# Projecting self-attention's values in PE tiles of 64 rows by 32 columns

## The chip, the cores and the metric

The kernel runs on one NeuronCore of a Trainium2 chip. Five engines work side by side, each with its own list of instructions: TensorE (PE in the profile, its weight loads PEld), VectorE (DVE), ScalarE (ACT), GpSimd (POOL) and SyncE (SP), which issues most DMAs. They wait for each other through semaphores only. The metric is the device time of one execution in microseconds (us). Before the change it is 1100.89 us, the median of three runs (1097.67, 1102.98 and 1100.89).

## The reference

A transformer block in float32 with batch 2, 1024 tokens of 256 features, and a context of 154 tokens of 192 features per batch. Self-attention, cross-attention and a gated feed-forward part follow each other, each behind a layer norm and with a residual sum:

```
h = layernorm(x, ln1);  x = attention(h, h, sa_wq, sa_wk, sa_wv, sa_wo, sa_bo) + x
h = layernorm(x, ln2);  x = attention(h, cond, ca_wq, ca_wk, ca_wv, ca_wo, ca_bo) + x
h = layernorm(x, ln3);  p = h @ ff_w1 + ff_b1
x = (p[:, :1024] * gelu(p[:, 1024:])) @ ff_w2 + ff_b2 + x
```

`attention` has 16 heads of 64: `q`, `k` and `v` are products with 256 x 1024 weights, the scores are scaled by 1/8 and go through a softmax, and the weighted values are multiplied by `wo`. The change is about one product alone, `v = h @ sa_wv` of self-attention.

## The kernel before

**Units and periods.** Self-attention goes by 16 units: 2 batches by 8 pairs of heads (128 columns of `q`, `k` and `v` each). A unit has eight periods (`for p in range(SA)` in the main loop, SA = 128 periods). In a period PE computes the scores of two groups of queries (`scores`, L482, matmuls at L489, tile `s`), then one block of other work: the weighted values of the half unit before (`weigh`, L528, matmuls at L535, tile `po`), or a projection for the next unit (`project_both`, L351, matmuls at L358: `pq_sa`, `pk_sa`; `project_self_values`, L383, matmuls at L389: `pv_sa`), and where there is room a piece of the output projection (L463, `py_sa`) or four transposes of a layer norm (L276, `ph_ln`). The order is written out by hand: `run_work` (L559) takes the next projection from a list, and the program's order on each engine is the order in which the Python code emits.

**Behind the scores.** DVE takes the maximum over each score tile (L650, tile `st`), ACT exponentiates (L500, tile `p`), SP exchanges the halves' maxima and sums by four small DMAs (L510), POOL joins and scales (L518 to L525, L600), and DVE transposes the weights (L614, tile `pT`) for `po`. There are two score tiles in PSUM, and a period uses both: the scores of the next period wait until ACT has read these.

**PE's tiles.** A matmul here names a tile of the array by rows (what is summed over) and columns (what comes out in PSUM's partitions); matmuls in different tiles can run side by side. Scores, `po`, `pq_sa` and `pk_sa` use tiles of 64 rows by 32 columns, eight in the array. `pv_sa` uses 64 rows by 128 columns, two in the array. Each has the two halves of the tokens in the two halves of the partitions: row tile `r` takes its 64 partitions of the normalised activations `h` and writes into its own PSUM bank `pv[r]`.

**The value projection.** For each of the four tiles of 128 tokens in a half (`i`) it sums over four chunks of 64 features (`c`, NH = 4), with the tokens as the stationary operand (128 columns) and 128 columns of `sa_wv` streamed past. That is 4 x 4 x 2 = 32 matmuls a unit. A float32 matmul shows as two records in the trace, one for each of two passes, each with its weight load: 64 records a unit, 1,024 in all. The first unit's block is done in two halves of two token tiles each. Then ACT copies both banks into `v_sa` (L398), and two DMAs (L405, L406) put the other half of the partitions beside. `po` of the next unit reads `v_sa`.

Of the kernel before, what the change touches and what calls it, by code (L numbers as in the profile page):

```python
# [13 lines left out]
P = 128  # L14
# [4 lines left out]
def tile_transformer_block(ctx: ExitStack, tc: tile.TileContext, a: dict, out: bass.AP):  # L19
    nc = tc.nc  # L20
# [15 lines left out]
    HR = P // 2  # L36
    NH = D // HR
    CC = DC // 2
    KP = T // 2
    KB = 32  # L40
# [56 lines left out]
    row_of, r = {}, 0  # L97
# [69 lines left out]
    for n in names[2:]:  # L167
        own = rows[row_of[n] - n_cols:row_of[n] - n_cols + n_of[n], :]
# [214 lines left out]
    def project_self_values(v, pv, wt, h, i0, n, soon):  # L383

        for i in range(i0, i0 + n):
            for c in range(NH):
                for r in range(2):
                    own = slice(r * HR, (r + 1) * HR)
                    nc.tensor.matmul(  # L389
                        pv[r][:, i * P:(i + 1) * P], lhsT=h[own, c, i * P:(i + 1) * P],  # L390
                        rhs=wt[own, c, :], start=(c == 0), stop=(c == NH - 1),
                        tile_position=(r * HR, 0),
                    )

        def store():
            tiles = [slice(r * GT + i0, r * GT + i0 + n) for r in range(2)]
            for r in range(2):
                nc.scalar.copy(  # L398
                    v[:, tiles[r], 0, :],
                    pv[r][:, i0 * P:(i0 + n) * P].rearrange("p (t d) -> p t d", d=P))  # L400
            if i0 + n == GT:
                move()

        def other_half():
            nc.sync.dma_start(out=v[:QG, :, 1, :], in_=v[QG:, :, 0, :])  # L405
            nc.sync.dma_start(out=v[QG:, :, 1, :], in_=v[:QG, :, 0, :])  # L406

        def move():
            if soon:
                other_half()  # L410
            else:
                later.append(other_half)

        return store
# [33 lines left out]
    def value_pieces(b, pr, parts, soon=True):  # L448
        n = GT // parts
        return [  # L450
            costing(2, lambda i=i: project_self_values(
                qk["sa", b, pr][2], two_banks(f"pv_sa{b}_{pr}_{i}"), wsl["sa", pr, "v"],
                hT["sa", b], i * n, n, soon))
            for i in range(parts)
        ]
# [626 lines left out]
    with tc.manual_schedule():  # L1082
# [11 lines left out]
        own = [ps_s.tile([P, 2, HB], F32, tag="s", name=f"first_{r}") for r in range(2)]  # L1094
# [45 lines left out]
        for p in range(SA):  # L1140
# [20 lines left out]
            h, hg = divmod(p, SH)  # L1161
            if h == 0 or hg < LAG:
# [5 lines left out]
                f = (ui - NPAIR // 2 - 1) * EC  # L1168
# [107 lines left out]
        for k in range(2 * FU):  # L1276
            c = CA + k
# [59 lines left out]
```

## Time and profile before

The profiled execution took 1098.87 us, and its span, from the first instruction of the program to the last, is 1097.1 us.

| what | busy us (share) | instructions |
|---|---|---|
| PE | 1076.0 (98%) | 18388 |
| PEld | 711.9 (65%) | 18388 |
| DVE | 893.2 (81%) | 1301 |
| ACT | 638.1 (58%) | 2057 |
| POOL | 730.1 (67%) | 1552 |
| `pv_sa` on PE (L389) | 62.0 | 1024 |
| scores on PE (L489) | 260.2 | 4096 |
| `po` on PE (L535) | 239.1 | 8192 |

Self-attention fills the span up to about 700 us, cross-attention overlaps its end, and the feed-forward part is last. A line of a group of instructions reads: source line, engine, operation, tile written and tiles read, for PE the tile of the array (`64*32` is 64 rows by 32 columns) and the streamed operand, the count; then busy time in us and the mean duration of one in ns; then the idle time before them and what ended it. Busy times are those of overlapping records taken together. A record's duration includes the time that a matmul needs to pass through the array, so that records of different tiles overlap, and costs are better read from the start of one block of matmuls to the start of the next.

### The profile page before, as it was taken

What the parts mean: (1) busy time and instruction counts of PE and PEld (TensorE: products, weight loads), DVE (VectorE), ACT (ScalarE), POOL (GpSimd) and SP (SyncE); (2) the same over time, 40 slices, a digit from 0 to 9 for tenths busy, and PEclk for the clock granted to TensorE, in tenths of its full rate; (3) what the DMA queues carried; (4) which work ended last, traced back from release to release, by engine and by line L of the source; (5) the groups of instructions that cost most, each with busy time, mean ns of one, the idle gap of its engine ahead of it and who ended that gap; (6) DMA issues with size and microseconds to landing.
All of it is one profiled execution on the core that took longest, in us unless ns stands there. A gap on an engine that the chain in (4) does not pass through costs nothing.

```text
span 1097.1 us, 44912 instructions
## 1 busy us (share of the span) xinstructions
PE 1076.0 (98%) x18388; PEld 711.9 (65%) x18388; DVE 893.2 (81%) x1301; ACT 638.1 (58%) x2057; POOL 730.1 (67%) x1552
## 2 busy tenths in 40 slices
PE   8999999999999999999999999899999999899998
PEld 6555656556766565566575666566766677688887
DVE  5888999898989998999999989978877877644442
ACT  5666766667666666666776775666555554232221
POOL 2676777777777777777776777776756785565331
PEclk9999999999999999999999999999999999999999
DMA  3222112122111011111110210136665545000000
GB/s 82 67 57 57 46 43 52 42 49 46 35 41 45 20 42 33 38 42 24 42 42 19 47 33 18 28 99 157 170 154 124 116 106 116 1 10 14 12 15 29
DMA packets 104094, 60.71 MB, mean 55 GB/s; under 512 B 32330, under 2 KB 94674, under 8 KB 103890
## 3 DMA queue, kind: packets, MB, share of 16 engines
q1 hardware_dynamic: 102514, 57.07, 21.9%
q8 instruction: 145, 2.38, 0.9%
q10 hardware_dynamic: 1376, 0.79, 0.2%
q14 instruction: 59, 0.48, 0.2%
HBM read 27.91 MB, written 2.10 MB: 27 GB/s over the span
## 4 chain that ended last, share of the span: by engine, by line
PE 72%; ACT 7%; DMA 5%; DVE 5%; POOL 5%; SPq 3%; issue 3%; DVEq 0%; POOLq 0%; ACTq 0%
PE po L535 14%; PE s L489 14%; ACT p L500 6%; PE pf L1065 5%; PE py_ca L463 5%; DMA st<-st 5%; PE py_sa L463 4%; PE pq_ca L358 4%; PE poc L877 4%; PE pb L999 4%; PE pv_sa L389 3%; PE pk_sa L358 3%; DVE st L650 3%; PE sc L798 3%; SPq L510 3%
## 5 line engine op out<-in xcount | busy, mean ns | idle before, releaser
L500 ACT ACTIVATE p<-s,st 128x512 f32<-128x512 f32 x512 | 344.8, 686 | 195.8 <-DVE st L650 183.2
L600 POOL TENSOR_SCALAR p<-p,rd,ee 128x512 f32<-128x512 f32 x512 | 385.7, 767 | 47.7 <-DVE rd L596 46.7
L650 DVE TENSOR_REDUCE st<-s 128x2 f32<-128x1024 f32 x256 | 300.7, 1215 | 23.6 <-PE s L489 11.1
L614 DVE STREAM_TRANSPOSE pT<-p 128x1024 f32<-128x1024 f32 x256 | 302.2, 1217 | 0.2 <-POOL p L600 0.2
L489 PE MATMUL s<-k_sa,q_sa 64*32 64x512 f32 x4096 | 260.2, 592 | 8.8 <-ACT p L500 7.8
L535 PE MATMUL po<-pT,v_sa 64*32 64x256 f32 x8192 | 239.1, 376 | 0.7 <-DVE pT L614 0.7
L535 PEld LDWEIGHTS po<-pT,v_sa 64*32 64x32 f32 x8192 | 173.5, 106 | 75.1 <-issue 20.3
L489 PEld LDWEIGHTS s<-k_sa,q_sa 64*32 64x32 f32 x4096 | 80.8, 106 | 114.3 <-ACT p L500 58.7
L814 ACT ACTIVATE p<-sc,neg 128x154 f32<-128x154 f32 x256 | 96.2, 405 | 84.2 <-DVE rden L822 81.0
L825 POOL TENSOR_SCALAR p<-p,rden 128x154 f32<-128x154 f32 x256 | 96.8, 398 | 59.4 <-DVE rden L822 58.9
L500 ACT ACTIVATION_READ_ACCUMULATOR p<-s,st 128x1 f32 x512 | 103.8, 203 | 0.0
L523 POOL TENSOR_TENSOR zz<-ee,st 128x8 f32<-128x8 f32 x128 | 25.9, 202 | 73.1 <-ACT ee L521 73.1
L389 PEld LDWEIGHTS pv_sa<-sa_wv,hT_ln 64*128 64x128 f32 x1024 | 58.8, 188 | 14.6 <-DMA sa_wq<-in_L_xattn_sa_wq_dram 5.0
L389 PE MATMUL pv_sa<-sa_wv,hT_ln 64*128 64x128 f32 x1024 | 62.0, 275 | 0.3 <-ACT v_sa L398 0.3
L463 PE MATMUL py_ca<-ca_wo,o_ca 128*128 128x256 f32 x256 | 60.0, 382 | 0.5 <-DVE o_ca L890 0.5
L518 POOL TENSOR_TENSOR dd<-st 128x8 f32<-128x8 f32 x128 | 25.5, 199 | 52.0 <-DMA st<-st 47.6
L463 PE MATMUL py_sa<-sa_wo,o_sa 128*128 128x256 f32 x256 | 59.7, 385 | 0.0
L463 PEld LDWEIGHTS py_sa<-sa_wo,o_sa 128*128 128x128 f32 x256 | 47.3, 190 | 17.8 <-issue 6.2
L358 PE MATMUL pq_sa<-hT_ln,sa_wq 64*32 64x512 f32 (+1 forms) x976 | 57.9, 586 | 0.0
L358 PE MATMUL pq_ca<-hT_ln,ca_wq 64*128 64x512 f32 (+1 forms) x304 | 57.8, 590 | 0.0
L803 DVE TENSOR_REDUCE neg<-sc 128x6 f32<-128x924 f32 (+1 forms) x48 | 47.8, 998 | 11.9 <-PE sc L798 11.8
L358 PE MATMUL pk_sa<-hT_ln,sa_wk 64*32 64x512 f32 x960 | 57.3, 591 | 0.0
(117 smaller groups left out, 1454.5 us busy)
## 6 DMA issues: line engine op xcount, KB each, us to landing
wf<-pT_ca SPq DMA_DIRECT2D x128, 128.0 KB, 2.4
st<-st SPq DMA_DIRECT2D x512, 1.0 KB, 1.8
v_sa<-v_sa SPq DMA_DIRECT2D x32, 256.0 KB, 3.8
sa_wq<-in_L_xattn_sa_wq_dram SPq DMA_DIRECT2D x32, 128.0 KB, 3.5
sa_wk<-in_L_xattn_sa_wk_dram SPq DMA_DIRECT2D x32, 128.0 KB, 2.9
sa_wv<-in_L_xattn_sa_wv_dram SPq DMA_DIRECT2D x32, 128.0 KB, 3.2
ca_wq<-in_L_xattn_ca_wq_dram SPq DMA_DIRECT2D x32, 128.0 KB, 3.9
wf<-in_L_xattn_ff_w_dram SPq DMA_DIRECT2D x12, 256.0 KB
```

What stands on the lines that cost most here:

```text
L358: nc.tensor.matmul(pq[r][f:f + m, at:at + n], lhsT=wt[own, c, f:f + m], rhs=h[own, c, t0:t0 + n], start=(c == 0), stop=(c == NH - 1), tile ...
L389: nc.tensor.matmul(pv[r][:, i * P:(i + 1) * P], lhsT=h[own, c, i * P:(i + 1) * P], rhs=wt[own, c, :], start=(c == 0), stop=(c == NH - 1), ...
L463: nc.tensor.matmul(py[:, e * D:(e + 1) * D], lhsT=o[:, i, (t + e) * P:(t + e + 1) * P], rhs=wo[kind][:, g * HP + i, :], start=(i == 0), st ...
L489: nc.tensor.matmul(sc[a4 * KB:(a4 + 1) * KB, j, :], lhsT=q[r, c:c + KB], rhs=k[r, h * HB:(h + 1) * HB], start=True, stop=True, tile_positi ...
L500: nc.scalar.activation(pr[:, j, :], sc[:, j, :], AF.Exp, bias=st[:, 0, 0, i, j:j + 1], accum_out=st[:, 0, 1, i, j:j + 1],)
L535: nc.tensor.matmul(po[a2][d:d + KB, :QH // 2], lhsT=v[r, t, e, d:d + KB], rhs=pT[r, d // DH * NK + n, :], start=(t == 0 and e == 0), stop= ...
L600: nc.gpsimd.tensor_scalar(pr[:, j, :], pr[:, j, :], rd[:, c:c + 1], ee[:, 0, c:c + 1], op0=ALU.mult, op1=ALU.mult,)
L614: nc.vector.transpose(halves[h][:, :, c:c + KB], groups.pop(0).rearrange("p j (n k) -> p (j n) k", k=KB))
L650: nc.vector.tensor_reduce(st[:, 0, 0, i, :], sc[i], AX.X, ALU.max, negate=True)
L814: nc.scalar.activation(pr_[:, j, i, :T], sc[:, j, i * T:(i + 1) * T], AF.Exp, bias=neg[:, j, i:i + 1], accum_out=den[:, j, i:i + 1],)
L825: nc.gpsimd.tensor_scalar(pr_[:, j, i, :T], pr_[:, j, i, :T], rden[:, j, i:i + 1], 1.0, op0=ALU.mult, op1=ALU.mult,)
L1065: nc.tensor.matmul(own[:, :D], lhsT=ub[pair][j][:, f, e * P:(e + 1) * P], rhs=w2[:, f, :], start=(f == 0), stop=(f == NF - 1),)
```

## The change

The matmuls of the value projection are cut into tiles of 64 rows by 32 columns: the 128 tokens of the stationary operand are loaded as four times 32 columns, and each quarter writes its 32 partitions of the same PSUM bank. The streamed operand, its 128 columns and the sum over `c` stay. There are four times as many matmuls, 128 a unit; the two row tiles and the four column tiles follow each other in the order that `project_both` has. Nothing else is changed: what the copies and DMAs behind it do is the same.

```
         for i in range(i0, i0 + n):
             for c in range(NH):
-                for r in range(2):
-                    own = slice(r * HR, (r + 1) * HR)
-                    nc.tensor.matmul(
-                        pv[r][:, i * P:(i + 1) * P], lhsT=h[own, c, i * P:(i + 1) * P],
-                        rhs=wt[own, c, :], start=(c == 0), stop=(c == NH - 1),
-                        tile_position=(r * HR, 0),
-                    )
+                for f in range(0, P, KB):
+                    for r in range(2):
+                        own = slice(r * HR, (r + 1) * HR)
+                        nc.tensor.matmul(
+                            pv[r][f:f + KB, i * P:(i + 1) * P],
+                            lhsT=h[own, c, i * P + f:i * P + f + KB],
+                            rhs=wt[own, c, :], start=(c == 0), stop=(c == NH - 1),
+                            tile_position=(r * HR, f),
+                        )
```

`P` is 128, `HR` 64 and `KB` 32.

## The prediction

> **What bounds the kernel now.** I read the page first, then the groups of instructions with shapes kept apart, the chain of waits through one stretch of the self-attention stage, the timeline around two value projections, the list of who waited for whom, and last a table of stretches between value projections.
>
> The page's busy times and the groups by shape:
>
> ```profile
> PE 1076.0 (98%) x18388; PEld 711.9 (65%) x18388; DVE 893.2 (81%) x1301; ACT 638.1 (58%) x2057; POOL 730.1 (67%) x1552
> ...
> L535 PE MATMUL po<-pT,v_sa 64*32 64x256 f32 x8192 | 239.1, 376 | 0.7 <-DVE pT L614 0.7
> L389 PE MATMUL pv_sa<-sa_wv,hT_ln 64*128 64x128 f32 x1024 | 62.0, 275 | 0.3 <-ACT v_sa L398 0.3
> ```
>
> PE is busy 98% of the span and waits almost nowhere, so its time is the first suspect. The changed line takes 62.0 us. Each float32 matmul of the code shows as two records: 512 calls stand behind the x1024.
>
> The chain of waits from 300 to 330 us (start, length, what), a stretch in which nothing but PE is on the chain:
>
> ```profile
> 302.62 3.77 PE pv_sa L389 x64
> ...
> 315.17 3.45 PE po L535 x128
> 318.63 1.72 PE s L489 x32
> ```
>
> These lengths are true costs, start to next start. A block in tiles of 64 rows by 32 columns (`64*32`) works through eight tiles side by side: scores, 32 records of 512 columns, are 4 groups of eight at 1.72 / 4 = 0.430 us; `po`, 128 records of 256 columns, is 16 groups at 3.45 / 16 = 0.2156 us. The value projection, 64 records of 128 columns in tiles of 64 rows by 128 columns (`64*128`), is 32 pairs at 3.77 / 32 = 0.118 us.
>
> The timeline of PE alone, at a value projection with scores on both sides:
>
> ```profile
> 43.93 1.93 PE L489 MATMUL s<-k_sa,q_sa 64*32 64x512 f32 x32
> 45.79 3.84 PE L389 MATMUL pv_sa<-sa_wv,hT_ln 64*128 64x128 f32 x64
> 49.56 1.95 PE L489 MATMUL s<-k_sa,q_sa 64*32 64x512 f32 x32
> 51.30 3.01 PE L535 MATMUL po<-pT,v_sa 64*32 64x256 f32 x104
> ```
>
> Scores ahead of the other shape last 45.79 - 43.93 = 1.86 us, those behind it 1.74, against 1.72 between blocks of one shape. So leaving `64*32` costs 0.14 us and entering it 0.02, beside what lies in the 3.77.
>
> Who waited for whom, 40 to 650 us (us in total, times, longest):
>
> ```profile
> ACT p L500 <- DVE st L650: 159.9, 103, 2.8
> ...
> PEld s L489 <- ACT p L500: 46.3, 88, 1.6
> ```
>
> PE's weight loads for the scores wait for the exponentials that still read the old scores, and these for the vector engine's maxima. Most of that is hidden behind the block that PE is running. Where it is not, the table of stretches shows it (PE, PEld, DVE, ACT, POOL busy us with counts, clock, DMA):
>
> ```profile
> 50.00:84.00 34.00, 33.20 (x864) 17.61 (x848) 29.60 (x31) 21.86 (x67) 23.84 (x52) 1.00 0.23 58
> 88.00:128.00 40.00, 38.99 (x912) 21.00 (x908) 36.32 (x42) 26.09 (x79) 28.29 (x61) 1.00 0.21 50
> 132.00:168.00 36.00, 36.00 (x866) 19.96 (x872) 34.63 (x42) 24.36 (x71) 27.27 (x56) 1.00 0.18 41
> ...
> 262.00:302.00 40.00, 40.00 (x936) 27.71 (x936) 35.54 (x40) 27.83 (x83) 30.71 (x65) 1.00 0.19 43
> ...
> 435.00:475.00 40.00, 39.87 (x924) 22.87 (x920) 38.27 (x45) 25.96 (x80) 28.79 (x62) 1.00 0.17 40
> ```
>
> Between the fifteen full blocks PE stands, in order of time, for 0.80, 1.01, 0, 0, 0.49, 0, 0, 0, 0.23, 0.13, 0.24, 0.02, 0.02 and 0 us; DVE is busy up to 38.27 of 40 us. There PE and DVE are nearly equal bounds. The granted clock is 1.00 throughout.
>
> **The change, part by part.**
>
> *Matmuls.* 512 calls become 2,048, so 1,024 records become 4,096; per block 64 become 256, which is 32 groups of eight tiles. The work streamed is the same: a tile's 128 columns pass 32 times either way. The trace has no `64*32` group of 128 columns, so I bound it. From below: the two rows above give (0.430 - 0.2156) / 256 = 0.84 ns a column and almost no fixed part, so 128 columns need 0.2156 - 128 x 0.00084 = 0.108 us. From above: the densest stream of `64*32` matmuls in the trace is `po`, 3.45 / 128 = 27 ns apiece; if the queue cannot issue faster, a group takes 8 x 27 = 0.216 us. Between them decides the one place where PE starts from rest behind a wait. The timelines of weight loads and matmuls from 17.6 us:
>
> ```profile
> 17.69 0.21 PEld L489 LDWEIGHTS s<-k_sa,q_sa 64*32 64x32 f32 x16 [0.81 <-ACT k_sa L381]
> 17.72 0.66 PE L489 MATMUL s<-k_sa,q_sa 64*32 64x512 f32 x8 [0.64 <-DVE k_sa L379]
> ```
>
> Each load lasts 0.106 us by the groups, so sixteen start within 0.21 - 0.106 = 0.10 us, and eight matmuls (0.61 us each here) within 0.05 us. A group of 128 columns needs eight of each in 0.108 us. That is nearer to the lower end; I take 0.1085 us, a block of 32 x 0.1085 = 3.47 us.
>
> Against this speaks the Trainium skill, "TensorE: Matmul & The Clock Gate", Part 1: matmul starts never come closer than about 25 ns, however few the columns. The eight starts within 0.05 us show that this doesn't hold between tiles of one group; whether it holds as a mean over 256 no row shows. By the skill's figure a group would be 8 x 25 = 200 ns and the whole 512 x (0.200 - 0.118) = 42 us slower on PE (an estimate from that page); by the rows above it is not.
>
> *Shape changes.* The 15 full blocks and two half blocks (the first unit's) all follow scores. Seven full ones are followed by scores: each had 0.14 + 3.77 + 0.02 = 3.93 us, and has 3.47: 0.46 us less, of which 0.02 us is rounding that I drop (0.44). Eight are followed by the transposes of the next layer norm (`128*128`), so leaving `64*32` is paid after the block instead of before it: 0.14 + 3.77 against 3.47 + 0.14, 0.30, taken as 0.28. A half block is 0.24 shorter. Sum on PE: 7 x 0.44 + 8 x 0.28 + 2 x 0.24 = 5.8 us.
>
> *What of it reaches the end.* Where PE already stands in the stretch behind a block, the exponentials and behind them DVE set the pace; what PE saves it then waits. I count a block's saving in full where the stretch up to the next block shows no idle PE (the blocks at 128, 170, 259, 303, 346 and 605 us: 0.44 + 0.28 + 0.28 + 0.28 + 0.44 + 0.28 = 2.0), half where it idles 0.02 us, or only at the end of the stage (518, 562 and 648 us: 0.42), and not where it idles 0.13 us or more (46, 84, 214, 389, 432, 475 us) nor in the first unit, whose half blocks are followed by waits for start-up work. Sum 2.4 us. The ends: nothing given back, 5.8; all given back, 0.
>
> *Moved work and queues.* The lists of DVE, ACT, POOL and SP instructions, with their waits, are the same; no DMA is added but instruction loading. The two copies out of PSUM (L398) wait for a block that ends 0.3 to 0.4 us earlier, and behind them is ACT work that PE does not wait for yet.
>
> *Instruction loading.* The page's instruction queue q8 brings 145 packets and 2.38 MB, 16 KB each; over PE's 36,776 records (two times 18,388) that is 254 records a packet, so I take it to be PE's. 6,144 more records are 24 packets more. A packet of `po` lasts 254 records, 3.4 us; in the new block it lasts 1.73 us. Should loading not keep up, PE starves inside the block. Lower end: nothing, as the trace shows no wait for it. Upper end: the difference of 1.7 us lost twice a block, 16 x 3.4 = 54 us. I take nothing, as the nearest row, `po`, runs without a gap, and scores of 1.72 us and 64 + 64 records lie between the dense blocks.
>
> **Sum.** The profiled execution took 1098.87 us (span 1097.1 and 1.8 around it): 1098.87 - 2.4 = 1096.5. The median of the runs, 1100.89, is 2.0 above it, so 1098.5.
>
> **The rivals.**
>
> 1. *Issue binds (slower).* If eight loads and eight matmuls take longer than the columns to stream, the group is as long as their issue. The 5.8 us saved are gone at 0.1085 + 5.8 / 512 = 0.120 us a group. At 0.15 us PE has 512 x 0.0415 - 5.8 = 15 us more work; what waits for exponentials now (PE's idle 3.0 us between the blocks, and the slack that comes with it) would hide up to 5: 1111 to 1116. At `po`'s 0.216 us it is 512 x 0.1075 - 5.8 = 49 us, less up to 15: 1135 to 1150. For it: no stretch of the trace issues this densely for over 0.1 us. Against it: the burst at 17.7 us.
> 2. *Nothing is given back (faster by half a per cent).* 5.8 us, 1095.1. For it: in the stretches without idle PE the whole machine moves with it. Against: six of fourteen stretches show PE standing already.
> 3. *All is given back, or instruction loading eats it.* 1100.9, up to 1106. For it: DVE at 38.27 of 40 us. Against: DVE was below PE in every stretch.
>
> **How the numbers follow.** What a measurement can tell from no change is about 0.5%, 5.5 us. My forecast (a part is kept) 0.48; rival 3, 0.14; rival 2, 0.12; rival 1, 0.26, spread from 0.12 to 0.216 us a group, so that 0.03 of it stays within half a per cent and some 0.12 lies below 1112. So faster 0.12, within 0.5% 0.65, slower 0.23. The range reaches from rival 2 with 1 us of spread, 1094, to 1112, which leaves out the farther half of rival 1. The forecast alone: 1096 to 1101.
>
> **What would show it.** `pv_sa` at 4,096 records with `64*32` 64x128; blocks of 3.47 us from start to next start; scores ahead of them at 1.72 instead of 1.86; PE's wait for exponentials up by some 3 us in the same stretches that have it now. Wrong if blocks last over 3.95 us, or if weight loads of `pv_sa` show idle time put down to issue.

## The result, and the profile after

The changed kernel takes 1125.39 us, the median of four runs (1123.58 to 1129.5), against 1100.58 us for the kernel before in the same comparison: 24.8 us more, a ratio of 1.0239 with a 95% interval of 1.0219 to 1.0258. The forecast was 1098.5 us and the range ended at 1112.

The page's busy times of the kernel after:

```profile
PE 1078.1 (96%) x21460; PEld 709.3 (63%) x21460; DVE 893.3 (80%) x1301; ACT 639.6 (57%) x2057; POOL 730.3 (65%) x1552
```

PE works 2 us longer in a span that is 25 us longer (1121.8 us), at a granted clock of 0.998. So the time has gone into standing still, and the groups of instructions with shapes kept apart, after, say where:

```profile
L390 PE MATMUL pv_sa<-sa_wv,hT_ln 64*32 64x128 f32 x4096 | 68.2, 271 | 23.9 <-issue 23.9
L390 PEld LDWEIGHTS pv_sa<-sa_wv,hT_ln 64*32 64x32 f32 x4096 | 61.0, 105 | 37.7 <-issue 34.7 <-DMA sa_wq<-in_L_xattn_sa_wq_dram 1.6 <-ACT v_sa L400 0.4
L400 ACT COPY v_sa<-pv_sa 128x512 f32<-128x512 f32 x30 | 16.2, 589 | 14.8 <-PE pv_sa L390 14.5
```

Before, PE stood 0.3 us ahead of `pv_sa`. Now it stands 23.9 us there, and no other engine and no DMA ends that idle time: it is put down to issue. ACT's copies, which used to find the block ready (the line of before follows), wait 14.5 us for it.

```profile
L398 ACT COPY v_sa<-pv_sa 128x512 f32<-128x512 f32 x30 | 16.1, 593 | 0.7 <-PE pv_sa L389 0.6
```

The timeline of PE, after, around one value projection (the count is that of the records in the row):

```profile
172.62 0.64 PE L491 MATMUL s<-k_sa,q_sa 64*32 64x512 f32 x8
173.05 3.32 PE L390 MATMUL pv_sa<-sa_wv,hT_ln 64*32 64x128 f32 x215
178.08 0.88 PE L390 MATMUL pv_sa<-sa_wv,hT_ln 64*32 64x128 f32 x41 [1.71 <-issue]
178.88 0.66 PE L276 MATMUL ph_ln<-ident,xn_ln 128*128 128x128 f32 x4
```

The first 215 matmuls stream as the forecast had it: (3.32 - 0.27) / 215 = 14.2 ns apiece, and start to start a group of eight takes 0.109 to 0.110 us wherever PE isn't stopped. Then PE stops for 1.71 us, and the rest comes. The block lasts 178.88 - 173.05 = 5.83 us in place of 3.77. Over the fifteen full blocks it is 4.5 to 6.4 us.

The chain of waits, after, from 128 to 140 us, shows two such stops in one block, and what lies between them:

```profile
127.64 1.43 PE s L491 x24
129.07 1.59 PE pv_sa L390 x113
130.66 0.47 issue
131.13 2.02 PE pv_sa L390 x128
133.14 1.44 issue
134.58 0.44 PE pv_sa L390 x13
```

Between the stops there are 128 matmuls, with their 128 weight loads 256 records: one packet of 16 KB of the instruction queue if a record stands for 64 bytes of it (16,384 / 256). This is not an accident of one block. Where PE's records are numbered from the start of the kernel (matmuls, weight loads and PE's own semaphore instructions), 21 of the 22 stops inside `pv_sa` fall on number 193 or 194 of a run of 256; the 22nd is the 2.3 us between the two halves of the first unit's block, in which PE does other work. At each of the 21 PE goes on 1.3 to 1.5 us after a packet of the queue has arrived, and the next packet starts 1.0 to 2.8 us after that. The page's row of this queue, after:

```profile
q8 instruction: 169, 2.77, 1.0%
```

There are 24 packets more than the 145 before, as forecast. The shortest time from the start of one packet to that of the next is 3.33 us, before it was 3.37. The value block now needs a packet every 1.73 us.

The waits of the same stretch, 40 to 650 us, after (us in total, times, longest):

```profile
PEld s L491 <- issue: 45.3, 157, 1.9
PEld pv_sa L390 <- issue: 29.1, 34, 2.0
...
PEld s L491 <- ACT p L502: 25.9, 55, 1.2
```

PE's wait for the exponentials, 46.3 us before, has gone down, not up by 3: PE now comes late, and finds the scores' tiles free. The loads of the scores, which stand behind seven of the fifteen blocks, wait for issue too: 45.3 us with one wait of 1.9, where before it was 27.6 us and none over 0.3. The stretches show the same turn (columns as before the change):

```profile
88.00:128.00 40.00, 39.09 (x970) 20.66 (x952) 35.70 (x41) 26.21 (x80) 27.40 (x58) 1.00 0.20 47
...
262.00:302.00 40.00, 38.72 (x1027) 22.12 (x1019) 34.24 (x38) 26.68 (x77) 28.60 (x57) 1.00 0.17 38
435.00:475.00 40.00, 37.53 (x1049) 21.89 (x1040) 36.69 (x43) 24.25 (x73) 28.70 (x60) 1.00 0.17 41
```

DVE falls from 38.27 to 36.69 of 40 us in the last of them: nothing behind PE has become the bound.

Two theories stood at this point, named F and I in what follows. F: PE gets no more than one packet of 256 records each 3.3 us or so, and starves in a block that uses them faster. I: loads and matmuls can't be issued this densely, whatever their loading. A second question was open beside it: would the smaller tiles have gained the 2.4 us that the forecast kept, if PE had not starved?

### The profile page after: what moved, and what is told of

Its sections match the earlier page's. It is cut to its first block, busy times and chain, and to the rows that moved or that the text cites. A ratio compares the mean times of both kernels' runs of the same rounds, so it can differ in the third digit from the quotient of the medians.

```text
span 1121.8 us, 51056 instructions
## 1 busy us (share of the span) xinstructions
PE 1078.1 (96%) x21460; PEld 709.3 (63%) x21460; DVE 893.3 (80%) x1301; ACT 639.6 (57%) x2057; POOL 730.3 (65%) x1552
## 4 chain that ended last, share of the span: by engine, by line
PE 75%; ACT 6%; DMA 5%; DVE 4%; issue 4%; POOL 4%; SPq 2%; DVEq 0%; ACTq 0%; POOLq 0%
PE s L491 15%; PE po L537 14%; PE pv_sa L390 5%; ACT p L502 5%; PE pf L1067 5%; PE py_ca L465 5%; DMA st<-st 4%; PE py_sa L465 4%; PE poc L879 4%; PE pq_ca L358 4%; PE pb L1001 3%; PE pk_sa L358 3%; PE pq_sa L358 3%; PE sc L800 3%; DVE st L652 2%
## 5 line engine op out<-in xcount | busy, mean ns | idle before, releaser
L537 PE MATMUL po<-pT,v_sa 64*32 64x256 f32 x8192 | 236.2, 376 | 0.7 <-DVE pT L616 0.7
L537 PEld LDWEIGHTS po<-pT,v_sa 64*32 64x32 f32 x8192 | 170.3, 106 | 77.6 <-issue 26.8
L390 PE MATMUL pv_sa<-sa_wv,hT_ln 64*32 64x128 f32 x4096 | 68.2, 271 | 23.9 <-issue 23.9
L390 PEld LDWEIGHTS pv_sa<-sa_wv,hT_ln 64*32 64x32 f32 x4096 | 61.0, 105 | 37.7 <-issue 34.7
L816 ACT ACTIVATION_READ_ACCUMULATOR p<-sc,neg 128x1 f32 x256 | 56.4, 220 | 0.0
```

Source lines behind the costliest of these rows:

```text
L390: nc.tensor.matmul(pv[r][f:f + KB, i * P:(i + 1) * P], lhsT=h[own, c, i * P + f:i * P + f + KB], rhs=wt[own, c, :], start=(c == 0), stop=( ...
L537: nc.tensor.matmul(po[a2][d:d + KB, :QH // 2], lhsT=v[r, t, e, d:d + KB], rhs=pT[r, d // DH * NK + n, :], start=(t == 0 and e == 0), stop= ...
L816: nc.scalar.activation(pr_[:, j, i, :T], sc[:, j, i * T:(i + 1) * T], AF.Exp, bias=neg[:, j, i:i + 1], accum_out=den[:, j, i:i + 1],)
```

## Experiments on the stops

**The same tiles with half the records.** The value projection in tiles of 64 rows by 32 columns, but 256 columns streamed by each matmul:

```
-        for i in range(i0, i0 + n):
+        for i in range(i0, i0 + n, 2):
             for c in range(NH):
+                c2 = min(c, NH - 2)
...
-                            pv[r][f:f + KB, i * P:(i + 1) * P],
+                            pv[r][f:f + KB, i * P:(i + 2) * P],
...
-                            rhs=wt[own, c, :], start=(c == 0), stop=(c == NH - 1),
+                            rhs=wt[own, c2:c2 + 2, :], start=(c == 0), stop=(c == NH - 1),
```

> The value projection keeps tiles of 64 rows by 32 columns, but streams 256 columns at a time: 1,024 calls instead of 2,048, the same time on the array (16 groups of 0.216 us a block), half the records (256 a block). Left out: the right sum; chunk c is multiplied with weight chunks c and c+1, so the values are not the reference's. Theory F (instruction loading: PE gets 256 records in no less than about 3.4 us): no gap inside the blocks, blocks of about 3.45 us, and the time is what I had forecast for the change, 1096 to 1100, some 2 to 3 us under the kernel before. Theory S (the 64 by 32 shape itself costs here, by weight loads, PSUM or lost clock): blocks stay at 4 us or more and the time over 1110. Theory D (what PE saves is lost at DVE and the exponentials, and more): 1100 or above with blocks of 3.45 us.

It took 1104.4 us, 1.0015 of the kernel before (0.9998 to 1.0032). The group of this kernel:

```profile
L391 PE MATMUL pv_sa<-sa_wv,hT_ln 64*32 64x256 f32 x2048 | 60.4, 376 | 0.5 <-ACT v_sa L401 0.5
```

No stop is left, and blocks last 3.45 us where scores follow at once. So the tiles, the order and the work streamed are innocent, and the number of records is what stops PE. But the saving of about 0.3 us a block does not show in the time: all of it is given back, where 2.4 us was forecast to stay.

**Tiles between the two.** 64 rows by 64 columns, twice the matmuls of before instead of four times (`for f in range(0, P, HR)`, with 64 columns in each load):

> The value projection in tiles of 64 rows by 64 columns: twice the calls of the kernel before (1,024), 256 records a block, 32 groups of four tiles. Theory F: 256 records in some 3.5 us just pass, no gap inside the blocks or one of a few tenths of a us; the change of tile shape is paid as before, so 1098 to 1103. Theory I (each matmul beyond those of before costs its issue, in proportion to their number): a third of the loss of the change for a third of its extra matmuls, 1106 to 1110.

1104.84 us, 1.0016 (0.9999 to 1.0034). Blocks last 3.655 us without a stop, with 256 records each. This is F's number, and also a correct kernel that is no better than before.

**The other way round: more records in `po`.** The kernel before, with the weighted values in two runs of 128 columns instead of one of 256:

```
-        for e in range(2):
+        for e, x in ((e, x) for e in range(2) for x in range(0, QH // 2, P)):
...
-                        po[a2][d:d + KB, :QH // 2],
-                        lhsT=v[r, t, e, d:d + KB], rhs=pT[r, d // DH * NK + n, :],
+                        po[a2][d:d + KB, x:x + P],
+                        lhsT=v[r, t, e, d:d + KB], rhs=pT[r, d // DH * NK + n, x:x + P],
...
```

Among the lines left out is the flag that starts a sum: it is set on the first of the two runs alone.

> The kernel before, with the value projection untouched, but the weighted values streamed in two runs of 128 columns instead of one of 256: 4,096 more calls, 8,192 more matmul records and as many loads, the same columns through the array. Theory F: a block of 512 records takes two loadings, about 6.9 to 7 us instead of 3.45; with the scores' 64 records a period has 576, which need 7.7 us instead of 5.17. Over 64 blocks 2.5 to 3.5 us each: 1260 to 1320. If only the value projection's place or data were slow: at most 1110.

1271.17 us, 1.1521 (1.1457 to 1.1585). Its group, and its instruction queue:

```profile
L535 PE MATMUL po<-pT,v_sa 64*32 64x128 f32 x16384 | 282.8, 272 | 120.3 <-issue 120.1
```

```profile
q8 instruction: 209, 3.42, 1.1%
```

64 packets more cost 1271.2 - 1103.3 (the kernel before in that comparison) = 168 us, 2.6 us each, with 120 us of stops put down to issue. The 64 `po` blocks of 512 records take 3.8 to 8.3 us, 6.0 in the median; with 1.72 us and 64 records of scores that is 2.25 packets in 7.7 us, 3.4 us each. The stops thus follow the records, not the value projection.

**Half of the sum.** The kernel after, with chunks 0 and 2 of the four alone, so that a block has 256 records in tiles of 64 rows by 32 columns with 128 columns:

```
-            for c in range(NH):
+            for c in range(0, NH, 2):
...
-                            rhs=wt[own, c, :], start=(c == 0), stop=(c == NH - 1),
+                            rhs=wt[own, c, :], start=(c == 0), stop=(c == NH - 2),
```

> The changed kernel with half of the sum left out (feature chunks 0 and 2 of four): blocks of 256 records, 16 groups of 0.109 us. Theory F: one boundary of 256 records lies in a block, and the records before it were sparse, so most blocks take 1.75 us and some up to 2.7; the streak of 27 ns a matmul does not hold. Theory I (a matmul costs at least 27 ns as a mean): every block takes 3.4 us or more. Total: F 1070 to 1090, as DVE gives part back; I 1095 to 1105.

1102.0 us in a single run. Half of the blocks last 1.94 to 2.33 us, so 256 records can be issued in less than 2 us: theory I, which needs 3.4, falls. The stops that are left are three, 0.36 to 1.29 us, at the same place of the packet. Yet F's 1070 to 1090 us is a miss. PE is busy 1057.9 us, 18 less than before, and the time stays. What limits the kernel where PE is quick had to be found by itself.

## Experiments on what gives the saving back

In the kernel before, in the one with 256 columns and in the one with half the sum, a unit of eight periods lasts 42 to 45 us alike (behind the first two), though their value blocks last 3.77, 3.45 and 1.9 to 3.5 us. The chain of waits of the kernel with 256 columns, at a stretch where PE is not on it for long:

```profile
366.61 0.59 SPq L513
367.25 0.59 SPq L513
367.88 3.63 DMA st<-st
371.68 0.21 POOL dd L521
371.97 0.26 POOL dd L522
372.25 0.22 ACT ee L524
372.54 0.21 POOL zz L526
372.82 0.21 POOL den L528
373.35 1.24 DVE st L653
374.61 1.16 ACT p L503 x3
```

It is a loop: SP issues the exchange of the softmax halves' maxima and sums (L513), the DMA lands, POOL and ACT join them in five small operations, DVE takes a reciprocal (0.17 us, in the gap between POOL's end at 373.03 and 373.35), and only then, in its order, the next maxima; ACT's exponentials follow, and free the scores' tiles for PE. The waits of before had two rows of it (40 to 650 us):

```profile
POOL dd L518 <- DMA st<-st: 30.2, 40, 1.9
DVE rd L596 <- POOL den L525: 24.9, 46, 1.7
```

Theory L says that this loop sets the pace where PE doesn't (L2, in the expectations, that it does so through the exchange); theory D, that DVE's or ACT's own busy time does.

**The reciprocal taken off DVE.** Four kernels, the one before, the one with 256 columns, the one after, and the one with 64 columns a tile, each with one line changed (`minus1` is a tile of -1.0):

```
-            nc.vector.reciprocal(rd, den)
+            nc.gpsimd.tensor_tensor(rd, den, minus1, ALU.pow)
```

> The kernel before with the four reciprocals a step of the softmax sums taken by POOL (a power of -1) instead of DVE (L596); nothing else. Three theories of what takes back the time that PE saves. L, a loop through the reciprocal: in the chain of waits of before (46.5 to 53.3 us) the sums' exchange, four small operations of POOL and ACT, DVE's reciprocal and behind it DVE's next maxima follow each other; between 40 and 650 us DVE stood 24.9 us (46 times) at the reciprocal for POOL. With the reciprocal off DVE its maxima no longer stand behind that: a third to two thirds of the 24.9 us come back, 8 to 16 us, 1087 to 1095. D, DVE's own work sets the pace: the reciprocal is 0.06 us of it a step, so 1099 to 1104, ratio 0.998 to 1.002. W, POOL's queue becomes late (POOL is busy 67% and now itself waits for the sums ahead of its scaling): 1105 to 1115.

> The kernel of e1 (value projection in 64*32 tiles of 256 columns, half the calls; chunk c meets the weights of chunks c and c+1, so the values are wrong sums) with the reciprocal on POOL as in e5. Beside e5 it shows whether the 0.3 us a block that the shape of the tiles saves on PE reach the end once DVE's maxima no longer wait behind the reciprocal. L: 2 to 6 us faster than e5. D: as e5 within 1.5 us, as e1 was as before. W: as e5, within 1.5 us.

> The kernel after with the reciprocal on POOL. If PE starves for instructions inside the blocks whatever DVE does, it stands as far behind e5 as after stood behind before, 20 to 30 us; the stalls inside the blocks are still 21 to 23, at the same place of each packet, and the shortest spacing of instruction packets is still 3.3 us. If instead the blocks were late for something that DVE or POOL hand over, the difference to e5 shrinks under 10 us.

> The kernel of e2 (value projection in tiles of 64 rows by 64 columns, twice as many matmuls) with the reciprocal on POOL. No stalls inside the blocks, blocks of 3.65 us as in e2. L: 1 to 3 us faster than e5, for 0.1 us less a block and a cheaper change of shape. D and W: as e5 within 1.5 us.

Measured: 1142.04 (ratio 1.036, 1.0342 to 1.0377), 1142.17 (1.0366, 1.0347 to 1.0385), 1148.66 (1.0432, 1.0408 to 1.0457) and 1140.96 us (1.0362, 1.034 to 1.0384); the kernel before took 1101.39. The groups of the first of them show why:

```profile
L598 POOL TENSOR_TENSOR rd<-den,minus 128x4 f32<-128x4 f32 x128 | 132.2, 1033 | 10.0
```

The power takes POOL 1033 ns for four numbers a partition, against 174 ns for DVE's reciprocal. So W came true, by more than it said: 0.86 us more a step cost 41 us over 128 steps, 0.32 us a step. That does not tell L from D, since POOL stands in the loop and was also busier. It does show that the join has little slack. The third kernel gave the second answer expected of it (less than 10 us): it stands 6.6 us behind the first instead of 24.8, although its stops are still there, 23 of them at record 193 or 194 of the packet, and packets come no closer than 3.38 us. A kernel held up elsewhere hides most of them.

**The exchange left out.** To take the loop's wait away without a slower operation, the four DMAs are dropped and the join reads the own half in place of the other's; the operations and their sizes stay:

```
     def exchange(st):
-        for a4 in range(4):
-            o4 = a4 ^ 1
-            nc.sync.dma_start(
-                out=st[a4 * KB:(a4 + 1) * KB, 1], in_=st[o4 * KB:(o4 + 1) * KB, 0]
-            )
+        return
...
-        neg = st[:, :, 0].rearrange("p s i j -> p s (i j)")
+        neg = st[:, 0].rearrange("p s i j -> p s (i j)")
...
-        nc.gpsimd.tensor_tensor(zz, ee, st[:, :, 1].rearrange("p s i j -> p s (i j)"), ALU.mult)
+        nc.gpsimd.tensor_tensor(zz, ee, st[:, 0].rearrange("p s i j -> p s (i j)"), ALU.mult)
```

> The kernel before without the exchange of maxima and sums between the halves of the keys: the four DMAs of L510 are left out, and the join on POOL reads the own half's maxima and sums in place of the other's (the weights are wrong, the operations and their sizes the same). L2, the loop that gives the saving back runs through the exchange (maxima on DVE, exponentials on ACT, the DMAs, the join, the reciprocal, the next maxima): with it out, PE no longer waits between the blocks, and the time falls by PE's idle time in the self-attention stage, 3 to 10 us, 1091 to 1098. D, DVE's and ACT's own work sets the pace and the exchange is hidden: 1099 to 1104.

> The kernel of e1 (64*32 tiles of 256 columns in the value projection, wrong sums) without the exchange, as in e9. L2: the saving of the tiles' shape now reaches the end, 3 to 6 us faster than e9. D: as e9 within 1.5 us, as e1 was as before.

> The kernel after without the exchange, as in e9 (wrong weights). PE's starving for instructions does not go through the exchange: blocks of 4 to 6.3 us with their stalls at the same place of the packets as in after, 20 to 30 us slower than e9. If the stalls cost less than that, by how much PE's idle time between the blocks covers them is read from the difference to 24.8.

Measured, with the kernel before at 1102.14: 1085.78 us (0.9854, 0.9837 to 0.987), 1081.41 (0.9815, 0.9799 to 0.9832) and 1116.21 (1.0126, 1.0101 to 1.015). The stretch from 42 to 650 us as one row, of the kernel before, of the first and of the second:

```profile
42.00:650.00 608.00, 604.80 (x13802) 362.52 (x13788) 559.60 (x626) 407.00 (x1204) 450.23 (x930) 1.00 0.18 41
```

```profile
42.00:650.00 608.00, 608.00 (x13990) 359.69 (x13980) 567.24 (x635) 415.04 (x1225) 458.11 (x947) 1.00 0.16 40
```

```profile
42.00:650.00 608.00, 608.00 (x15089) 368.76 (x15076) 571.17 (x641) 417.30 (x1233) 460.62 (x953) 1.00 0.17 41
```

With the exchange out PE never stands: 608.00 of 608 us, and DVE gets through more work in the same time (567 us instead of 560), so DVE was no bound. The time falls by 16.4 us, more than the 3 to 10 expected from PE's idle time. And now the tiles' shape counts: tiles of 32 columns with 256 streamed are 4.4 us faster than tiles of 128 columns, within the 3 to 6 expected. D is out.

The two profiled executions differ by 13.4 us (1098.87 against 1085.50). Where were the other 10, if PE stood for only 3.2 us before? The scores' group, of the kernel before and then of the kernel without the exchange:

```profile
L489 PE MATMUL s<-k_sa,q_sa 64*32 64x512 f32 x4096 | 260.2, 592 | 8.8 <-ACT p L500 7.8
```

```profile
L489 PE MATMUL s<-k_sa,q_sa 64*32 64x512 f32 x4096 | 248.8, 591 | 4.5 <-ACT p L500 3.9
```

The same 4,096 matmuls, at the same 592 ns each, keep PE busy 11.4 us less. A record lasts 0.59 us while the next starts 0.054 us later (1.72 us for 32). When the next has to wait, the earlier ones are still in the array, and up to half a microsecond of waiting is counted as busy time. In the kernel before blocks of scores of 2.2 us stand beside those of 1.72. The saving of the 256 columns with the exchange in place is found at the same spot: there the scores' matmuls are busy 263.6 us with 11.0 us idle before them, 5.7 us more in sum than in the kernel before.

The third kernel, after's tiles without the exchange, is 30.4 us slower than the first, just above the 20 to 30 expected. That is the net cost of the change where the exchange covers nothing. The stops (19 of its 20 at the same place of the packet, packets never closer than 3.31 us) are most of it: the fifteen full blocks last 81.3 us against 56.6 in the first kernel, 24.7 more. Where the other 6 us arise no run tells.

**Two queues for the exchange.** The kernel before, with every second DMA of L510 issued by ACT instead of SP:

> The kernel before with two of the four DMAs of the exchange issued by ACT's queue and two by SP's; nothing is left out. L2: the last of the four starts 1.4 us earlier (SP's four issues take 2.8 us), so it is faster by 1 to 5 us. D: 1099 to 1104. A third way: ACT waits for its own sums ahead of its issues, and its exponentials come later, 1104 to 1112.

1109.32 us (1.0069, 1.0052 to 1.0085): the time of the third way, but not its reason. PE's loads wait less for the exponentials than before (16.8 us against 46.3). Instead PE stands 6.7 us ahead of `pk_sa`, where it did not stand before: 3.4 us are put down to ACT's copies of `q_sa`, 3.3 to DMAs of the exchange. ACT's issues seem to delay its copies; this was not tried by itself.

**The exchange kept, without DMAs.** Leaving it out had taken away a wait, 512 DMAs and the right weights at once. Two kernels do the same exchange by copies of 32 partitions, on POOL at the head of the join, and on ACT behind the exponentials (`nc.gpsimd.tensor_copy` and `nc.scalar.copy` in place of `nc.sync.dma_start`):

> The kernel before with the exchange done by four copies of 32 partitions on POOL at the head of the join, instead of four DMAs; nothing is left out. e9 took away the wait for the exchange, its DMAs and the right weights at once. L2, the loop's length is what counts: four copies of 0.1 to 0.2 us in place of 1.8 to 3.7 us of transfer and SP's issues, so 3 to 12 us faster than before, 1090 to 1098. W, POOL's longer work takes it back: e5's 0.86 us more a step on POOL cost 41 us, so at 0.6 us a step 1105 to 1130.

> The kernel before with the exchange done by four copies of 32 partitions on ACT behind a step's exponentials, instead of four DMAs; nothing is left out. L2: ACT's small operations take 0.21 us, so the exchange is done 0.85 us after the sums, where the DMAs took 1.8 to 3.7 and SP's issues before them: 5 to 14 us faster than before, 1088 to 1097. W: ACT's copies stand ahead of its other work, as its issues did in the kernel with two queues: 1103 to 1112.

On POOL 1158.11 us (1.0489, 1.0469 to 1.0509): W again, and more than its 1105 to 1130, for four copies of 184 ns a step. On ACT 1097.87 us against 1103.41 (0.9946, 0.9931 to 0.9961): a correct kernel that is half a per cent faster, at the weak end of what was expected, since ACT pays:

```profile
L510 ACT COPY st<-st 32x8 f32<-32x8 f32 x512 | 99.8, 195 | 7.5
```

On this kernel the tiles were tried again: 64 columns a tile, the kernel after's tiles, and 256 streamed columns.

> The value projection in tiles of 64 rows by 64 columns, as in e2, with the exchange on ACT, as in e18; nothing is left out. If the wait in the loop gave the saving back, the 0.1 us a block and the cheaper change of shape now show: 1 to 3 us faster than e18, 1095 to 1097. If ACT's 0.8 us more a step has become the loop's new end, as e18.

> The kernel after with the exchange on ACT; nothing is left out. If the DMAs of the exchange delay the instruction packets, the stalls in the blocks shrink, under 15 us behind e18. If PE's rate of consuming instructions alone makes them, the same stalls at the same place, 24 to 31 us behind e18, with the shortest spacing of packets still 3.3 us.

> The kernel of e1 (64*32 tiles of 256 columns, half the calls, wrong sums) with the exchange on ACT. If e18 has taken the wait out of the loop: 3 to 5 us faster than e18, as e10 was 4.4 faster than e9. If ACT's copies leave the loop as long as PE's work: as e18 within 1.5 us.

Measured, with the kernel before at 1102.31: 1095.67 us (0.994, 0.9919 to 0.996), 1125.61 (1.0217, 1.0191 to 1.0243) and 1093.17 (0.9918, 0.9899 to 0.9937). By the medians that is 2.2 us faster, 27.7 slower and 4.7 faster than 1097.87, all three as expected. The comparison with the kernel before was made anew for these three; by the ratios they differ from 0.9946 by -0.7, +29.9 and -3.1 us, and the interval of the 64-column kernel overlaps that of its base widely, the one of 256 columns by a little (0.9931 to 0.9937). So the 2 us are not shown, and the 3 to 5 are likely, in line with the 4.4 without the exchange. The waits in the kernel with 256 columns are small now, against 59.9 and 29.0 us in the same tiles with the DMAs:

```profile
PEld s L492 <- ACT p L503: 11.4, 24, 0.7
DVE rd L599 <- POOL den L528: 6.3, 17, 0.6
```

So what gave the saving back in these kernels is the loop through the exchange. The stops don't depend on the exchange's DMAs: 21 of 23 at the same place, the shortest spacing 3.30 us.

The four pairs put the net cost of the change side by side:

| beside | net cost of the change, us |
|---|---|
| the kernel before | 24.8 |
| the same, exchange left out | 30.4 |
| the same, exchange on ACT | 27.7 |
| the same, reciprocal on POOL | 6.6 |

The 64-column tiles with the exchange on ACT, 1095.67 us, is the fastest correct kernel of this study; it beats both the kernel before and the kernel after.

## Why the prediction was wrong

**The step that failed: instruction loading.** The prediction counted the 24 packets rightly, named the mechanism (PE starves inside the block), put its ends at 0 and 54 us, and then said "I take nothing, as the nearest row, `po`, runs without a gap". The row was read the wrong way. `po` uses a packet of 256 records in 3.45 us, and packets came no closer than 3.25 us in any run (3.37 before): `po` runs without a gap because it goes at about the rate at which packets can come, and is no evidence for twice that rate. The spacing of the packets themselves, which the trace of before holds, would have shown that nothing in it had been fed faster, though not that nothing could be. The second reason, that scores lie between the dense blocks, fails by a sum as well: 64 records of scores (32 matmuls and 32 loads, where the prediction has 64 + 64) and 512 of the block are 2.25 packets, 2.25 x 3.37 = 7.6 us, for 1.72 + 3.47 = 5.2 us of work. 2.4 us are short, of which what had been loaded ahead covers a part. Measured, the 21 stops sum to 29.6 us (each from the last start ahead of it to the next), 1.85 us for each of the 16 units. The term was 0 in the sum and is 29.6; the upper end was nearly twice too high. The chance of 0.23 for slower stood on rival 1 alone, which is not what happened.

The Trainium skill, "Runtime: NRT & Kernel Launch", section "Instruction fetch mechanics", has the blocks of 16 KiB and 256 instructions that the trace shows, and says that the next is fetched while the current one runs and that crossing costs little. In these runs it cost 1.4 us a stop on the mean, and 2.6 us for each packet added to `po`; here the measurement decides.

**Matmuls: right.** A group takes 0.109 us wherever records are at hand, so the lower bound held and rival 1, issue, is not what happened, though it named the symptom (idle time put down to issue) and ends near the measured time if 0.17 us a group is put in. The floor of some 25 ns between matmul starts that the prediction weighed (the Trainium skill, "TensorE: Matmul & The Clock Gate", Part 1) doesn't bind between tiles: 215 matmuls went by at 14.2 ns.

**Shape changes: right in kind.** Scores ahead of the block take 1.716 us instead of 1.86. Of the 5.8 us summed on PE, 4.4 showed where nothing else limited (without the exchange).

**What reaches the end: wrong.** 2.4 us were kept because stretches without idle time of PE were taken as PE's own pace. With the stops gone and the shape kept (256 columns) none of it came. PE's idle time understates its waiting: 3.2 us idle in 608, but 16.4 us came out when the wait was taken away (with the exchange's DMAs and the right weights; 5.5 us with copies on ACT in their place). And the engine named as pacing PE, DVE by its busy share, was not it; the loop through the exchange was, which the list of waits had shown in parts (`POOL dd` for `DMA st<-st`, 30.2 us; `DVE rd` for `POOL den`, 24.9).

**Rivals.** The third, "instruction loading eats it", was the right mechanism with a wrong size: it was let go up to 1106 where its own upper bound reached further. The signs to watch for were the right ones: blocks beyond 3.95 us, and weight loads of `pv_sa` idle by issue.

## What to carry to other kernels

Before cutting matmuls into smaller tiles, count PE's records per microsecond in the new block (loads included, two of each per float32 matmul) and compare it with the closest spacing of instruction packets in the trace: a row that runs without a gap at that spacing may be at the limit, and is no evidence for a faster rate. An engine's idle time is a lower bound of what it waits, since overlapping records hide short waits; compare the busy time of the same instructions, or their start-to-start times, with an undisturbed block. And a saving on the busiest engine is worth only what the slowest loop behind it lets through, which an experiment that removes one wait of that loop tells better than busy shares.

## What the runs showed of the hardware

- The closest packets of PE's instruction queue stood 3.25 to 3.51 us apart in the nineteen kernels (3.25 with the cut `po`), about 13 ns a record, while PE can use them at 7 (one load and one matmul in 13.7 ns). Taking 512 other DMAs away did not change that (3.31 us).
- In the changed kernel a packet took 0.9 to 1.4 us, so the spacing is not the transfer alone: behind a stop the next one started only 1.0 us or more after PE had gone on, and PE went on 1.3 us or more after a packet's arrival. The shortest of the three sum to 3.2 us, close to the closest spacing of 3.33 (an estimate from these rows). Why the next packet starts so late, no run here tells.
- POOL's power took 1033 ns on 128x4 numbers, DVE's reciprocal 174. Copies of 32x8 took 184 ns on POOL and 195 on ACT.
- The exchange by copies cost 55 us with 0.73 us more a step on POOL, and gained 5.5 us with 0.78 us more a step on ACT; the DMAs were dropped in both. That POOL's place between the exchange and its four scalings makes the difference is likely, and was not tried.
